# Graph attention and graph convolution on one core: three places for whole-array work in each batch instead of six

## The chip, the cores and the metric

The kernel runs on one core of a Trainium2 chip. The metric is the device time of one execution in microseconds (us). All data are 32-bit floats.

## The reference

`x` is (16, 1024, 256): 16 batches, 1024 nodes, 256 features. `adj` is (1024, 1024). Layer 0 is an attention whose queries come from a graph product, layer 1 a graph convolution with two linear layers and batch norms.

```python
# layer 0, with fea = x transposed to (b, c, n)
c_adj = mean(fea, axis=1)                              # mean of a node's features
diff  = c_adj[:, None, :] - c_adj[:, :, None]
A     = abs(abs(sigmoid(diff) - 0.5) - 0.5) * 2.0
Wg    = adj * (A + A.transpose(0, 2, 1)) * 0.5
g     = relu(einsum('bcn,bnm->bcm', fea, Wg) * para)
q     = g, as 4 heads of 64;   k, v = split(x @ kv_w)
out   = softmax(q k^T * scale) v
x     = layernorm(x + out)
# layer 1
A_hat = (adj + I) * dinv[:, None] * dinv[None, :]      # dinv = rsqrt(degree)
h     = relu(batchnorm((A_hat @ x) @ W1.T + b1))
x     = layernorm(x + batchnorm(h @ W2.T + b2))
```

## The kernel before

The function `fast_path` does the work in four stages: attention for all batches, aggregation with the first linear layer (with a seven-product scheme for block matrices), the second linear layer, and the final residual and layernorm. The change is in the first.

**The pieces of a batch.** The 1024 nodes lie as 8 chunks of 128. `prologue(b)` makes three lists of small steps for batch `b`, which the caller works off later:

- `first`: four `transpose_x(c, half)`, each of four 128x128 transposes on TensorE (tile `pxT`) and a copy to `xT`; the first of them also calls `begin`, which sums `x` on VectorE (`csum`), writes the negative means to memory and reads them back as a row on all partitions (`crow`).
- `side`: for each of 8 chunks `weights_abs` and `weights_tanh` on ScalarE and `weights_adj` on VectorE. They build the graph weights `wg` of 128x1024. That makes 24 steps.
- `steps`: four `values` (tile `pv`) and four `keys` (`pk`), and then `graph_mm`, the product of `x` with the 8 `wg` chunks (`pg`). At the end of each quarter `queries` multiplies with `para` on VectorE and applies Relu on ScalarE.

The profile counts each matmul of 32-bit data twice, so one quarter of `graph_mm` with its 8 matmuls is x16.

**The attention itself.** A unit is one batch, one pair of heads, one half of the queries (`qh`) and one chunk of keys (`m`). `scores(i)` makes the transposed scores of a unit (tile `ps`, from 64x64 quarters of the array) and their exponential `p` on ScalarE. `outputs(i)` multiplies `p` with the values (`po`, 64x64 quarters too) and sums `p` into `acc` on VectorE. A burst is two units; a batch has 16 bursts, with index `u` 0 to 15 in the batch. In each burst TensorE first makes the scores of burst `j` and then the outputs of burst `j-1` (`back`).

After each pair of heads `normalise` sums `acc` over partitions on TensorE (`den`, columns of 32), copies it on ScalarE (`drow`) and sends it through memory on SP's queue to come back as columns (`dcol`). `residual` takes the reciprocal, transposes the output (`poT`), multiplies (`o`) and adds to `x` on GpSimd. `finish_x1` does the layernorm and stores the result as `x1`.

**What sets the order.** The order on TensorE, ScalarE and VectorE is the order in which the loop emits the instructions (`manual_schedule`). Before the change whole-array work stands at these bursts, four steps at a time:

```python
FULL = (0, 4, 6, 8, 10, 12)
SIDE = {13: 2, 14: 2, 15: 2, 1: 2, 2: 2, 3: 2}
```

So `u` 0 and 4 hold values and keys (with two `side` steps behind each), and 6, 8, 10 and 12 one quarter of `graph_mm` each. 10 and 12 also take the transposes of the batch after next. `normalise` follows at the end of `u` 8 and, for the second pair, of `u` 0 of the next batch; the two `residual` of a pair four bursts later (`u` 12 and 4), `finish_x1` at `u` 5. The input of batch `b+2` is requested at `u` 5. In the last batch the free places hold the transposes of `adj` (`pah`) and of the layer-1 weights (`pw`).

**Buffers.** In PSUM the pool `s` has two tiles of two banks (scores), `t` two of one bank (`pxT`, `pv`, `pk`, `pg`, `den`, `poT`), and `o` two of one bank (`po`). In SBUF `p` has four buffers, `acc` two, `oT` three, `o` and `drow` one each, `x` three, `xT` and `crow` one, `wg` eight.

Of the kernel before, what the change touches and what calls it, by code (L numbers as in the profile page):

```python
# [18 lines left out]
P = 128  # L19
# [496 lines left out]
def fast_path(  # L516
# [86 lines left out]

    def products(name, bank, out, mm, temps, bias):
# [95 lines left out]
    with (  # L700
# [5 lines left out]
        tc.tile_pool(name="op", bufs=3) as op,  # L706
# [26 lines left out]
        def prologue(b):  # L733
# [24 lines left out]
            def transpose_x(c, half):  # L758
                if c == 0 and half == 0 and b:
                    begin()  # L760
# [7 lines left out]
                nc.vector.tensor_copy(s["xT"][:, c, half * HALF : (half + 1) * HALF], pt)  # L768
# [28 lines left out]
            def graph_mm(c, half, part):  # L797
                if part == 0:
                    s["pg"] = tile_t(f"pg_{b}_{c}_{half}")
                    if c == 0 and half == 0:  # L800
                        s["qT"] = qkv.tile([P, CC, N], F32, tag="qT", name=f"qT_{b}")
                ps = s["pg"]
                hs = slice(half * HALF, (half + 1) * HALF)
                for n in (2 * part, 2 * part + 1):
                    nc.tensor.matmul(  # L805
                        ps, xt[:, n, c * P : (c + 1) * P], s["wg", n][:, hs],
                        start=(n == 0), stop=(n == NCH - 1),
                    )
                if part == 3:
                    queries(c, hs, ps)  # L810
# [37 lines left out]
            def values(pair):  # L848
# [3 lines left out]
                for j in range(2):  # L852
# [6 lines left out]
                nc.vector.tensor_copy(  # L859
                    s["v"][:, 2 * pair : 2 * pair + 2, :].rearrange("p n c -> p (n c)"), pt  # L860
                )
# [3 lines left out]
            if b == 0:  # L865
                first += [(begin, ()), (row_of_means, ())]
            for i in range(4):
                step(values, i)
                step(keys, i // 2, i % 2)
            for c in range(CC):  # L870
                for half in range(2):
                    for part in range(4):
                        if b:
                            step(graph_mm, c, half, part)
# [105 lines left out]

        def finish_x1(b):
            xt = st.pop(b)["x"]
            layernorm(xt, f"l0_{b}")
            nc.gpsimd.dma_start(x1_d[b], xt)
# [125 lines left out]

        BURST = 2
        bursts = [range(i, i + BURST) for i in range(0, len(units), BURST)]
        PERB = PER // BURST
        FULL = (0, 4, 6, 8, 10, 12)
        SIDE = {13: 2, 14: 2, 15: 2, 1: 2, 2: 2, 3: 2}
        with tc.manual_schedule(engines={mybir.EngineType.PE, mybir.EngineType.Activation, mybir.EngineType.DVE}):
# [8 lines left out]
            run(next_first, 4)  # L1125
# [7 lines left out]
            full, sums, late = {}, {}, {}  # L1133

            def back(j):
# [4 lines left out]
                if m == NCH - 1 and qh == 1:  # L1140
                    sums.setdefault(j + 1, []).append((normalise, (b, pr)))
                    for q in range(2):
                        full.setdefault(j + 5, []).append((residual, (b, pr, q)))
                    if pr == PAIRS - 1:
                        late.setdefault(j + 6, []).append((finish_x1, (b,)))
# [14 lines left out]
                6: [(adjacency_rows, (n,)) for n in (0, 1, 2)] + [(load_weights, ())],  # L1160
                8: [(adjacency_rows, (n,)) for n in (3, 4, 5)],
                10: [(adjacency_rows, (n,)) for n in (6, 7)],
                12: [(adjacency_diagonal, ())],
            }
            for j in range(len(bursts)):
# [8 lines left out]
                run(late.get(j, []), 9)  # L1174
# [3 lines left out]
                if u in FULL:  # L1178
                    if u >= 10:
                        run(next_first, 1)  # L1180
                    for _ in range(4 if b or u > 4 else 0):
                        run(steps, 1)
                        if u <= 4:
                            run(side, 2)
                    if u >= 10:
                        run(next_first, 1)
                    run(full.get(j, []), 9)
                elif u > 12:
                    run(next_side, SIDE[u])
                else:  # L1190
# [441 lines left out]
```

## Time and profile before

| | |
|---|---|
| median of 3 runs | 2637.98 us (2637.81 to 2638.22) |
| the profiled execution | 2637.64 us, span 2635.9 us, mean TensorE clock 0.996 |
| TensorE matmul busy | 2572.7 us, 98% of the span |
| VectorE busy | 1587.8 us, 60% |
| ScalarE busy | 1110.2 us, 42% |
| GpSimd busy | 338.9 us, 13% |
| exponentials (512 on ScalarE) | 495.6 us, 1020 ns each |
| sums of `p` (384 of the 448 on VectorE) | 483.2 us, 1258 ns each |

The profile is of one execution. Times are from the start of its span. A group of instructions is written with its line, engine, operation, output and inputs, and count; in a timeline the first column is the start and the second the length. Matmuls overlap in the array and their ends are modelled, so distances between starts are the safer reading. A bracket gives the idle time of the engine before the group and what ended it. The queue of a wait is told as "engine line waited for: total us, times, longest us".

### The profile page before, as it was taken

The page shows a single profiled execution, that of the slowest core. Times are in us where ns is not written, and L with a number is a line of the kernel's source. Part 1 is how long each engine was busy: PE and PEld are TensorE (multiplying, and loading weights), DVE is VectorE, ACT ScalarE, POOL GpSimd, SP SyncE. Part 2 cuts the span into 40 slices and gives each one's busy share as a digit, 9 for nine tenths or more (in the row PEclk, how much of TensorE's full clock was granted, in tenths as well). Part 3 has the DMA queues.
Part 4 walks back from the last instruction along what each step waited for, and adds up shares of the span by engine and source line. Part 5 has one row for each costly group of instructions (what it writes and reads, how often), then busy time and mean ns, then how long its engine had stood idle before and what let it go on. Part 6 is the DMA issues. An engine that isn't in the chain of part 4 may idle for free. (4 is left out here: it accounts for less than half of the span.)

```text
span 2635.9 us, 32325 instructions
## 1 busy us (share of the span) xinstructions
PE 2572.7 (98%) x13158; PEld 1118.6 (42%) x13158; DVE 1587.8 (60%) x2159; ACT 1110.2 (42%) x1321; POOL 338.9 (13%) x407
## 2 busy tenths in 40 slices
PE   8999999999999999999999999999999999999986
PEld 4443444444434444444344443334444444444455
DVE  5465665756656657566566576766565565533367
ACT  5363563644635636546356364501100111133358
POOL 0001000100000001001000010232221122000036
PEclk9999999999999999999999999999999999999999
DMA  4001101011011010110110110112222222254458
GB/s 144 2 9 41 33 10 41 17 25 33 9 41 33 10 41 19 23 33 9 41 33 9 41 49 2 41 55 89 96 76 84 86 90 96 96 201 150 159 194 303
DMA packets 134557, 168.96 MB, mean 64 GB/s; under 512 B 86784, under 2 KB 120064, under 8 KB 124032
## 3 DMA queue, kind: packets, MB, share of 16 engines
q1 hardware_dynamic: 129568, 116.47, 14.1%
q0 software_dynamic: 4832, 50.34, 4.6%
q8 instruction: 105, 1.72, 0.3%
q14 instruction: 52, 0.43, 0.0%
HBM read 99.36 MB, written 67.44 MB: 63 GB/s over the span
## 5 line engine op out<-in xcount | busy, mean ns | idle before, releaser
L908 ACT ACTIVATE p<-ps 128x1024 f32<-128x1024 f32 x512 | 495.6, 1020 | 179.7 <-PE ps L903 132.6
L933 DVE TENSOR_TENSOR acc<-acc,p 128x1024 f32<-128x1024 f32 x384 | 483.2, 1258 | 60.9 <-ACT p L908 32.3
L903 PE MATMUL ps<-qT,kT 64*64 64x512 f32 x4096 | 490.5, 594 | 1.4 <-ACT p L908 1.4
L924 PE MATMUL po<-p,v 64*64 64x512 f32 x4096 | 485.3, 589 | 0.0
L805 PE MATMUL pg<-wg,x 128*128 128x512 f32 x960 | 425.2, 596 | 0.0
L979 POOL TENSOR_TENSOR x<-x,o 128x512 f32<-128x512 f32 x64 | 109.5, 1711 | 1434.8 <-DVE o L974 1434.8
L924 PEld LDWEIGHTS po<-p,v 64*64 64x64 f32 x4096 | 156.7, 133 | 282.8 <-issue 282.6
L805 PEld LDWEIGHTS pg<-wg,x 128*128 128x128 f32 x960 | 177.6, 190 | 226.9 <-issue 203.3
L903 PEld LDWEIGHTS ps<-qT,kT 64*64 64x64 f32 x4096 | 146.1, 132 | 280.2 <-issue 231.5
L817 ACT ACTIVATE qT<-qT 128x512 f32<-128x512 f32 x64 | 40.1, 630 | 481.9 <-DVE qT L814 481.9
L1457 PE MATMUL po<-hl,w12T 128*128 128x512 f32 x512 | 222.0, 596 | 3.6 <-ACT hl L1387 2.8
L814 DVE SCALAR_TENSOR_TENSOR qT<-pg,para_s 128x512 f32<-128x512 f32 x64 | 43.9, 689 | 270.7 <-PE pg L805 269.8
L793 DVE SCALAR_TENSOR_TENSOR wg<-wg,adj_s 128x1024 f32<-128x1024 f32 x128 | 153.1, 1217 | 16.0 <-ACT wg L789 16.0
L1457 PEld LDWEIGHTS po<-hl,w12T 128*128 128x128 f32 x512 | 97.7, 191 | 127.9 <-issue 120.4
L784 ACT ACTIVATE wg<-crow,ccol 128x1024 f32<-128x1024 f32 x128 | 146.6, 1146 | 12.2 <-DMA crow<-c 12.2
L789 ACT ACTIVATE wg<-wg 128x1024 f32<-128x1024 f32 x128 | 135.5, 1059 | 2.6
L1387 ACT ACTIVATE hl<-hl,bn_sh,bn_sg 128x1024 f32<-128x1024 f32 x64 | 74.4, 1229 | 137.4 <-DMA hl<-h 136.1
L855 PE MATMUL pv<-kvw_s,xT 128*128 128x256 f32 x512 | 124.0, 385 | 1.6 <-ACT kT L846 1.6
L1468 DVE TENSOR_SCALAR o<-po,col_b 128x1024 f32<-128x1024 f32 x31 | 39.8, 1283 | 138.1 <-PE po L1457 138.1
L842 PE MATMUL pk<-xT,kvw_s 128*128 128x512 f32 x256 | 120.3, 592 | 0.0
L855 PEld LDWEIGHTS pv<-kvw_s,xT 128*128 128x128 f32 x512 | 94.9, 190 | 51.9 <-issue 27.6
L1286 PE MATMUL b_agg<-aT,x1S 128*128 128x512 f32 x240 | 109.2, 598 | 0.0
(159 smaller groups left out, 2641.4 us busy)
## 6 DMA issues: line engine op xcount, KB each, us to landing
h<-hw POOLq DMA_DIRECT2D x16, 2048.0 KB, 6.6
hl<-h SPq DMA_DIRECT2D x15, 2048.0 KB
x<-x POOLq DMA_DIRECT2D x16, 1024.0 KB, 4.2
x1l<-x SPq DMA_DIRECT2D x16, 1024.0 KB
xf<-x SPq DMA_DIRECT2D x16, 1024.0 KB
out_dram<-o SPq DMA_DIRECT2D x16, 1024.0 KB
x<-in_x_dram SPq DMA_DIRECT2D x15, 1024.0 KB
crow<-c SPq DMA_DIRECT2D x15, 512.0 KB
```

The lines of the kernel that those rows point to most:

```text
L784: nc.scalar.activation(w, s["crow"], AF.Abs, bias=s["ccol"][:, n : n + 1])
L789: nc.scalar.activation(w, w, AF.Tanh, scale=0.5)
L793: nc.vector.scalar_tensor_tensor(w, w, 1.0, adj_s[:, n, :], op0=ALU.subtract, op1=ALU.mult)
L805: nc.tensor.matmul(ps, xt[:, n, c * P : (c + 1) * P], s["wg", n][:, hs], start=(n == 0), stop=(n == NCH - 1),)
L842: nc.tensor.matmul(ps, kvw_s[:, c, kc * P : (kc + 1) * P], s["xT"][:, c, hs], start=(c == 0), stop=(c == CC - 1),)
L855: nc.tensor.matmul(pt[:, j * C : (j + 1) * C], s["xT"][:, c, n * P : (n + 1) * P], kvw_s[:, c, C : 2 * C], start=(c == 0), stop=(c == CC - 1),
L903: nc.tensor.matmul(ps[kh * D : (kh + 1) * D, hd * HALF : (hd + 1) * HALF], kT[r, pr, ks], qT[r, pr, qh * HALF : (qh + 1) * HALF], start=Tr ...
L908: nc.scalar.activation(p, ps, AF.Exp)
L924: nc.tensor.matmul(g["po"][kh][hd * D : (hd + 1) * D, :], s["v"][r, m, h * D : (h + 1) * D], p[r, hd * HALF : (hd + 1) * HALF], start=(m = ...
L933: nc.vector.tensor_add(g["acc"], g["acc"], p)
L979: nc.gpsimd.tensor_tensor(xs, xs, o.rearrange("p n h d -> p n (h d)"), ALU.add)
L1457: nc.tensor.matmul(ps[:, hs], w2T[:, k, c * P : (c + 1) * P], h[k][:, hs], start=(k == 0), stop=(k == HC - 1),)
```

## The change

Whole-array work of a batch now stands at `u` 0, 4 and 8 only.

- `u` 0: seven of the eight value and key steps, two `side` steps behind each; `normalise` of the second pair of the batch before behind the second of them, and all four `residual` of that batch behind the third, fourth and sixth and at the end.
- `u` 4: the layernorm statistics of the batch before, then the first half of `graph_mm`, the layernorm's application in the middle of it, and the last key step.
- `u` 8: `begin` and two transposes of the batch after next, the second half of `graph_mm` with the other two transposes in its middle, and `normalise` of the first pair.
- `u` 9 to 15: one or two `side` steps behind each burst, ten in all; the other fourteen are those of `u` 0.

`graph_mm` now works on one 128-feature half with both halves of the columns, into a tile of the pool `s`; `queries` takes all 1024 columns at once. Half of the `xT` and `v` copies go to ScalarE (not for batch 0). The layernorm behind the attention is split by `layernorm_steps`: statistics on VectorE, two more small operations on GpSimd, and the application on ScalarE instead of VectorE. `oT` has four buffers. In the last batch the leftovers are placed by hand, and the row sums of `adj` are spread over more bursts of the batch before it.

```diff
+    def layernorm_steps(t, name):
+        st = small.tile([P, NCH, 6], F32, tag="ln_st", name=f"st_{name}")
+        mv = small.tile([P, NCH, 2], F32, tag="ln_mv", name=f"mv_{name}")
+        rstd = small.tile([P, NCH], F32, tag="ln_rs", name=f"rs_{name}")
+        nmr = small.tile([P, NCH], F32, tag="ccol", name=f"nm_{name}")
+        def statistics():
+            for n in range(NCH):
+                nc.vector.bn_stats(st[:, n, :], t[:, n, :])
+                nc.vector.bn_aggr(mv[:, n, :], st[:, n, :])
+            rsqrt(rstd, mv[:, :, 1], EPS)
+            nc.gpsimd.tensor_tensor(nmr, mv[:, :, 0], rstd, ALU.mult)
+            nc.gpsimd.tensor_scalar(nmr, nmr, -1.0, None, ALU.mult)
+        def apply():
+            for n in range(NCH):
+                nc.scalar.activation(
+                    t[:, n, :], t[:, n, :], AF.Identity,
+                    bias=nmr[:, n : n + 1], scale=rstd[:, n : n + 1],
+                )
+        return statistics, apply
...
-        tc.tile_pool(name="op", bufs=3) as op,
+        tc.tile_pool(name="op", bufs=4) as op,
...
             def transpose_x(c, half):
-                if c == 0 and half == 0 and b:
-                    begin()
...
-                nc.vector.tensor_copy(s["xT"][:, c, half * HALF : (half + 1) * HALF], pt)
+                copy = nc.scalar.copy if half and b else nc.vector.tensor_copy
+                copy(s["xT"][:, c, half * HALF : (half + 1) * HALF], pt)
...
-            def graph_mm(c, half, part):
-                if part == 0:
-                    s["pg"] = tile_t(f"pg_{b}_{c}_{half}")
-                    if c == 0 and half == 0:
+            def graph_mm(c, n):
+                if n == 0:
+                    s["pg"] = tile_s(f"pg_{b}_{c}")
+                    if c == 0:
                         s["qT"] = qkv.tile([P, CC, N], F32, tag="qT", name=f"qT_{b}")
-                ps = s["pg"]
-                hs = slice(half * HALF, (half + 1) * HALF)
-                for n in (2 * part, 2 * part + 1):
+                for hs in (H0, H1):
                     nc.tensor.matmul(
-                        ps, xt[:, n, c * P : (c + 1) * P], s["wg", n][:, hs],
+                        s["pg"][:, hs], xt[:, n, c * P : (c + 1) * P], s["wg", n][:, hs],
                         start=(n == 0), stop=(n == NCH - 1),
                     )
-                if part == 3:
-                    queries(c, hs, ps)
+                if n == NCH - 1:
+                    queries(c, slice(0, N), s["pg"])
...
-                nc.vector.tensor_copy(
-                    s["v"][:, 2 * pair : 2 * pair + 2, :].rearrange("p n c -> p (n c)"), pt
-                )
+                copy = nc.scalar.copy if pair % 2 and b else nc.vector.tensor_copy
+                copy(s["v"][:, 2 * pair : 2 * pair + 2, :].rearrange("p n c -> p (n c)"), pt)
...
+            else:
+                first.insert(0, (begin, ()))
...
-            for c in range(CC):
-                for half in range(2):
-                    for part in range(4):
-                        if b:
-                            step(graph_mm, c, half, part)
+            for c in range(CC if b else 0):
+                for n in range(NCH):
+                    step(graph_mm, c, n)
...
+        def statistics_x1(b):
+            statistics, st[b]["ln"] = layernorm_steps(st[b]["x"], f"l0_{b}")
+            statistics()
         def finish_x1(b):
-            xt = st.pop(b)["x"]
-            layernorm(xt, f"l0_{b}")
-            nc.gpsimd.dma_start(x1_d[b], xt)
+            s = st.pop(b)
+            s["ln"]()
+            nc.gpsimd.dma_start(x1_d[b], s["x"])
...
-        FULL = (0, 4, 6, 8, 10, 12)
-        SIDE = {13: 2, 14: 2, 15: 2, 1: 2, 2: 2, 3: 2}
...
-            run(next_first, 4)
+            run(next_first, 5)
...
                 if m == NCH - 1 and qh == 1:
-                    sums.setdefault(j + 1, []).append((normalise, (b, pr)))
+                    sums.append((normalise, (b, pr)))
                     for q in range(2):
-                        full.setdefault(j + 5, []).append((residual, (b, pr, q)))
+                        full.append((residual, (b, pr, q)))
                     if pr == PAIRS - 1:
-                        late.setdefault(j + 6, []).append((finish_x1, (b,)))
+                        late.append((statistics_x1, (b,)))
+                        late.append((finish_x1, (b,)))
...
             before_last = {
-                6: [(adjacency_rows, (n,)) for n in (0, 1, 2)] + [(load_weights, ())],
-                8: [(adjacency_rows, (n,)) for n in (3, 4, 5)],
-                10: [(adjacency_rows, (n,)) for n in (6, 7)],
-                12: [(adjacency_diagonal, ())],
+                6: [(load_weights, ())],
+                8: [(adjacency_rows, (n,)) for n in (0, 1, 2, 3)],
+                10: [(adjacency_rows, (4,))],
+                11: [(adjacency_rows, (5,))],
+                12: [(adjacency_rows, (6,))],
+                13: [(adjacency_rows, (7,))],
+                15: [(adjacency_diagonal, ())],
             }
...
                 if j:
                     back(j - 1)
-                run(late.get(j, []), 9)
                 if u == 5 and b + 2 < B:
                     load_x(b + 2)
                     next_first, next_steps, next_side = prologue(b + 2)
-                if u in FULL:
-                    if u >= 10:
-                        run(next_first, 1)
-                    for _ in range(4 if b or u > 4 else 0):
+                if b == B - 1:
+                    if u == 0:
+                        run(sums, 1)
+                    elif u in (2, 4, 12):
+                        run(full, 2)
+                    elif u == 5:
+                        run(late, 1)
+                    elif u == 7:
+                        run(late, 1)
+                    elif u == 8:
+                        run(sums, 1)
+                elif u == 0:
+                    for i in range(7):
+                        if b:
+                            run(steps, 1)
+                            run(side, 2)
+                        if i == 1:
+                            run(sums, 1)
+                        if i in (2, 3, 5):
+                            run(full, 1)
+                    run(side, 99)
+                    run(full, 1)
+                elif u == 4:
+                    run(late, 1)
+                    keys_last = steps[:1] if b else []
+                    del steps[: len(keys_last)]
+                    for n in range(NCH):
                         run(steps, 1)
-                        if u <= 4:
-                            run(side, 2)
-                    if u >= 10:
-                        run(next_first, 1)
-                    run(full.get(j, []), 9)
-                elif u > 12:
-                    run(next_side, SIDE[u])
-                else:
-                    run(side, SIDE.get(u, 0))
+                        if n == 3:
+                            run(late, 1)
+                    run(keys_last, 1)
+                elif u == 8:
+                    run(next_first, 3)
+                    for n in range(NCH):
+                        run(steps, 1)
+                        if n == 3:
+                            run(next_first, 2)
+                    run(sums, 1)
+                elif u > 8:
+                    run(next_side, 2 - u % 2)
                 if b == B - 2:
                     run(before_last.get(u, []), 9)
                 if b == B - 1:
                     run(last.get(u, []), 9)
-                run(sums.get(j, []), 9)
             j = len(bursts)
             back(j - 1)
             for m in range(NCH):
                 if m + 1 < NCH:
                     scale_adjacency(m + 1)
                 aggregate_first(m)
-                run(sums.get(j + m - 1, []), 9)
-                run(full.get(j + m, []), 9)
+                if m == 1:
+                    run(sums, 1)
+                if m == 4:
+                    run(full, 2)
             for i in range(NCH // 2):
                 adjacency_sums(i)
-            run(late.get(j + 5, []), 9)
+            run(late, 2)
```

More of the change, by code (lines that the diff above doesn't have):

```diff
@@ L1132, in fast_path @@
             run(next_steps, 8)
-            full, sums, late = {}, {}, {}
+            full, sums, late = [], [], []
             def back(j):
```

## The prediction

> **What bounds the kernel now.** I read the page's busy times first, then the instructions of TensorE in order of time over one middle batch, then its waits, then the other engines beside it.
>
> ```profile
> PE 2572.7 (98%) x13158; PEld 1118.6 (42%) x13158; DVE 1587.8 (60%) x2159; ACT 1110.2 (42%) x1321; POOL 338.9 (13%) x407
> PEclk9999999999999999999999999999999999999999
> ```
>
> TensorE has something in flight 98% of the span at full clock, so only what makes its instructions stand further apart than their work needs can be won. Busy time hides that, so I take starts. In the timeline of PE the columns are start, length, and group:
>
> ```profile
> 514.59 1.90 PE L903 MATMUL ps<-qT,kT 64*64 64x512 f32 x16
> 516.30 1.90 PE L924 MATMUL po<-p,v 64*64 64x512 f32 x16
> 518.13 7.13 PE L805 MATMUL pg<-wg,x 128*128 128x512 f32 x16
> 525.19 1.95 PE L903 MATMUL ps<-qT,kT 64*64 64x512 f32 x16
> 526.96 1.90 PE L924 MATMUL po<-p,v 64*64 64x512 f32 x16
> 528.68 1.90 PE L903 MATMUL ps<-qT,kT 64*64 64x512 f32 x16
> ...
> 547.80 7.03 PE L805 MATMUL pg<-wg,x 128*128 128x512 f32 x16
> 554.67 0.60 PE L765 MATMUL pxT<-ident,x 128*128 128x128 f32 x4
> ...
> 590.89 1.88 PE L842 MATMUL pk<-xT,kvw_s 128*128 128x512 f32 x4
> 592.70 1.06 PE L946 MATMUL den<-acc,ones 128*32 128x512 f32 x8
> 593.70 1.95 PE L903 MATMUL ps<-qT,kT 64*64 64x512 f32 x16
> ```
>
> Half a burst (ps or po, in 64*64 quarters of the array) takes 1.71 to 1.72 from start to start. The po before whole-array work takes 1.83 (516.30 to 518.13), 0.12 more. Sixteen pg take 7.06 if ps follows (518.13 to 525.19), and 6.87 if another whole-array group follows (547.80 to 554.67): 0.19 more. The first ps afterwards takes 1.77, 0.05 more. So one block of whole-array work between bursts costs 0.12+0.19+0.05 = 0.36 us beyond its work. A den (columns of 32) behind pk costs 0.10: 1.81 against the 1.71 between pk groups.
>
> Check on a whole batch: 16 bursts x 3.43 = 54.9; pg 4 x 6.87 = 27.5; eight value and key groups x 1.715 = 13.7; two den at 0.9, four pxT at 0.5, four poT at 0.55 = 6.0; waits 0.59; six blocks x 0.36 = 2.2. The sum is 104.9; the trace has 104.90 (pv at 502.69 to pv at 607.59). Nothing is left unexplained, and what can be won is blocks and waits, 2.8 us a batch.
>
> The waits of PE inside the attention part, and beside them the order on ACT in a block that holds keys and weights:
>
> ```profile
> PE poT L970 <- DVE qT L814: 5.2, 15, 0.3
> PE poT L970 <- ACT kT L846: 3.4, 14, 0.2
> PE ps L903 <- ACT p L908: 1.4, 2, 1.1
> ```
>
> ```profile
> 589.37 0.58 ACT L846 COPY kT<-pk 128x512 f32<-128x512 f32 x1 [2.09 <-PE pk L842]
> 589.85 1.15 ACT L784 ACTIVATE wg<-crow,ccol 128x1024 f32<-128x1024 f32 x1
> ```
>
> poT waits for one of the two buffers of the pool `t`: 0.24 when ACT must first empty the pk two groups earlier, 0.35 behind DVE's qT.
>
> **The change, part by part.**
>
> Blocks. Before: 4 in batch 0 (u 6, 8, 10, 12), 6 in each of batches 1 to 14, 6 in batch 15 = 94. After: 2 + 14 x 3 + 7 (poT alone at u 2 is a new one) = 51. 43 fewer x 0.36 = **15.5 us less**. Matmuls, weight loads and transposes stay the same in number.
>
> The den of the second pair moves from the end of a block to its inside (k, den, v). Leaving whole-array work into den is paid before and after; new is the return to v. Not shown before; nothing at least, 0.36 at most; the nearest row is the 0.10 of pk to den, with 0.1 more for a first pv (1.83 against 1.73): 0.2 x 14 = **2.8 more**. Here the Trainium skill (TensorEngine Tiling (Array Packing), Key Properties) says that changing the tiling mode drains TensorE, while another tile of the same mode does not. It agrees with transposes costing no step beside pg. Taken strictly, a 32-column den amid 128-column work is a full extra change, 0.36 x 14 = 5.0, and the forecast would be 2628.0. I take the row.
>
> Waits. The old 0.59 a batch goes (8.6 in all). In the new first block the order on `t` is v0, k0, den, v1, poT, k1, poT, v2, k2, poT, v3, poT. Three places have the known shape "ACT empties it, one poT in between": k1 behind v1, v2 behind k1, v3 behind k2, 0.24 each. ACT's order is abs, k0, tanh, drow, v1, abs, tanh, k1, abs, tanh, k2, abs, tanh, v3. From starts ACT takes 1.15 for an abs, 0.97 for a tanh, 0.48 for a copy. Laid against PE's 1.72 groups, ACT is free 0.9 before v1 is ready, 0.1 late for k1, 1.5 early for k2. So 0.72+0.1 = 0.82 x 14 = 11.5: **2.9 more** net. DVE's four o products now lie 2 to 4 us apart, so the single o buffer (POOL's 1.7 us add) no longer holds DVE; PE did not wait for that except in batch 15. dcol of the second pair: at the end of the attention DVE found it 3.9 us after the end of drow (1718.59 to 1722.51, the only DMA wait of that kind); here 8 us lie between.
>
> Weights and later DMAs. Ten side steps move to u 9 to 15: 1.2 us of ACT a burst beside 1.81 of exp, under 3.43. The oT copy fits too. begin now stands ahead of the third block. On SP, c to crow took 10.5 us from issue to issue (29.00 to 39.46) and 3.9 to land: with csum behind oT on DVE, crow lands about 18.3 us after the block starts, and ACT asks for it at 19.9. Cost nothing; cover 1.6 us, then some 0.5 before exp of the next burst is late. SP's den writes stand behind crow, ready at about the same time. The x load goes out behind the x1 store (u 5): store lands about 17 us after block two starts, the load took 5 us, x is needed at 29.5.
>
> Layernorm in two steps. DVE keeps 4.3 us of statistics, ACT gets eight Identity of 128x256. The nearest row, the same form with an SBUF source at the end (L1570), has 606 ns: 4.85 us at most; DVE's apply took 2.67. Against this stands the Trainium skill (ScalarE: Activation LUTs, Rules for kernel authors): use VectorE rather than ScalarE for multiply and add; its What ACT_TABLE_LOAD costs gives 280 + 0.833 N ns, 3.95 for eight as an estimate. By the rule the move loses 1.3 to 2.2 a batch, some 25 in all and 2651, if ACT were the limit there. It is not: block two keeps PE at pg and k3 for 15.6 us, in which ACT has only oT, this, one Relu and one copy, under 7 us. Nothing on the path. If that cover were gone, 4 us a batch. POOL's two new small operations (some 0.24 each) precede it.
>
> pg in pool `s` takes one of the two score buffers; its last matmul to the second score of the next burst is 1.73+0.86 (block two, k3 between) or 1.0+0.86 (block three, den between), the qT product of 1024 columns about 1.28 plus 0.2. Hidden by 0.4 at least. exp starts late behind Relu and drow in block three, but its buffers come free 0.5 before PE asks. xT and v copies on ACT lie in these slacks.
>
> Last batch. The exp held 3.94 by DVE's whole layernorm (1.08 on PE) goes; instead the ACT apply at u 7 holds exp and the adjacency copies about 1.5: **0.4 more**.
>
> End of attention:
>
> ```profile
> 1759.95 1.57 PE L1318 MATMUL b_h<-tT,w12T 128*128 128x512 f32 x2 [1.88 <-DVE u_h L615]
> 1761.31 4.90 PE L1286 MATMUL b_agg<-aT,x1S 128*128 128x512 f32 x8
> ```
>
> ```profile
> 1756.57 2.67 DVE L600 TENSOR_SCALAR x<-x,mv_l,rs_l 128x256 f32<-128x256 f32 x8 [2.11 <-POOL rs_l L589]
> 1759.15 0.74 DVE L615 SCALAR_TENSOR_TENSOR u_h<-b_h,col_b,p_h 128x512 f32<-128x512 f32 x1
> ```
>
> DVE waited for POOL and applied batch 15's layernorm ahead of u_h, and PE stood 1.88. That goes; ACT's agg copy is some 3.6 late instead, and its next reader is later still. Right after, eight b_agg took 4.74 to the next start instead of 3.43 (PEclk 0.57 from 1760 to 1764): 1.7 with b_h. Whether the dip goes too is open; half: 1.9+0.85 = **2.75 less**.
>
> Sum: -15.5 +2.8 +2.9 +0.4 -2.75 = -12.15. The profiled execution took 2637.64 (span 2635.9), 0.34 under the median of 2637.98, which I take as base: **2625.8**.
>
> **Rivals.**
> (a) The 0.36 is only partly per block, for instance because the ends of longer blocks stand further behind: half saved, 7.7, net 4.4: 2633.6. For it: the profile models matmul ends. Against: the batch sum closes at 104.9.
> (b) Slower: ACT paces the first block. If exp or weights leave ACT so far behind that two of the three copies (k1, k2) come one tanh (1.06) later, PE waits 2.1 more in 14 batches, 29.7: 2655. Deciding point: my gain of 0.7 a batch is gone once ACT is 0.8 late at k1. For it: only 0.1 of slack there. Against: ACT idles about 1.8 before k0.
> (c) The new waits don't come, den inside is free and the dip goes: 15.5+8.6+3.6 = 27.7, 2610. Against: the 0.24 was paid 14 times in this shape.
>
> **How the numbers follow.** My case 0.75, own range 2619 to 2631 (the bounds of den and dip, some 0.4 a batch on waits); (a) 0.12; (b) 0.08; (c) 0.05. 0.2%, 5.3 us, is what a measurement tells from no change; (a) lies within it. Faster 0.81, same 0.11, slower 0.08. The range 2617 to 2634 reaches into (a) and leaves out (b) and (c).
>
> **What would show it.** Right: a batch of about 104.15 from first pv to first pv; PE waits for ACT of 0.2 to 0.3 at k1, v2 and v3; no wait at poT; pg 13.7 for 32; no PE wait for u_h. Wrong: ps waiting for exp after block one or three, abs waiting for crow, or x late at the third block.

## The result and the profile after

The changed kernel takes 2630.41 us, the median of 12 runs (2629.23 to 2632.20), against 2637.52 for the kernel before, which ran beside it. The ratio is 0.9976, with a 95% interval of 0.9969 to 0.9984. The forecast was 2625.8, with a range of 2617 to 2634. The gain is 7.1 us where 12.15 were forecast: the sign held, the size came out at 0.6 of it. By its time alone the kernel lies nearer to rival (a) (2633.6) than to the forecast; what tells them apart are the timelines. The profiled execution has a span of 2628.9 us (2635.9 before).

The engines' busy times say little, as before:

```profile
PE 2565.4 (98%) x13158; PEld 1130.2 (43%) x13158; DVE 1515.3 (58%) x1941; ACT 1202.5 (46%) x1479; POOL 362.0 (14%) x439
```

VectorE went from 1587.8 to 1515.3 and ScalarE from 1110.2 to 1202.5, which is the layernorm's second half on its new engine and the shared copies. TensorE fell by 7.3, which is the size of the gain but does not show where it came from. For that I set stage starts from the timelines of TensorE against each other (us). A batch begins with its first `ps`. For batch 15 of the changed kernel, whose first `ps` come in pieces, the piece of twelve is taken (1621.88; the first single one starts 0.43 earlier). The last two starts are those of the first `pagg` and of the group behind the `b_agg` that follows the wait for `u_h`; the stretch between them, from the attention to the next stage, is the handover:

| stage | before | after | difference |
|---|---|---|---|
| first `ps` of batch 0 (prologue) | 75.46 | 75.86 | +0.40 |
| batch 0 | 86.99 | 85.25 | -1.74 |
| each of batches 1 to 13 | 104.90 | 104.41 | -0.50, together -6.47 |
| batch 14 | 104.45 | 103.48 | -0.97 |
| batch 15, to the first `pagg` | 77.57 | 81.76 | +4.19 |
| handover: `pagg` to the group behind that `b_agg` | 57.81 | 53.97 | -3.84 |
| from there to the end | 869.81 | 871.32 | +1.51 |

About 1 us of batch 0's gain and of batch 15's loss is the same work: the `poT` of each first pair moved on by one batch. The sum is -6.9, the difference of the spans (2635.86 and 2628.93). The middle batches fall short, the last batch loses, and the handover gains more than forecast.

First a middle batch: block one in the timeline of PE after the change (start, length, group, and the wait before it in brackets).

```profile
477.87 1.99 PE L877 MATMUL pv<-kvw_s,xT 128*128 128x256 f32 x8
479.70 1.88 PE L864 MATMUL pk<-xT,kvw_s 128*128 128x512 f32 x4
481.51 1.06 PE L967 MATMUL den<-acc,ones 128*32 128x512 f32 x8
482.51 1.99 PE L877 MATMUL pv<-kvw_s,xT 128*128 128x256 f32 x8
484.34 0.60 PE L991 MATMUL poT<-ident,oT 128*128 128x128 f32 x4
485.18 1.98 PE L864 MATMUL pk<-xT,kvw_s 128*128 128x512 f32 x4 [0.24 <-ACT v L882]
487.00 0.60 PE L991 MATMUL poT<-ident,oT 128*128 128x128 f32 x4
487.83 1.99 PE L877 MATMUL pv<-kvw_s,xT 128*128 128x256 f32 x8 [0.24 <-ACT kT L868]
489.67 1.88 PE L864 MATMUL pk<-xT,kvw_s 128*128 128x512 f32 x4
491.38 0.60 PE L991 MATMUL poT<-ident,oT 128*128 128x128 f32 x4
492.22 1.99 PE L877 MATMUL pv<-kvw_s,xT 128*128 128x256 f32 x8 [0.24 <-ACT kT L868]
494.05 0.60 PE L991 MATMUL poT<-ident,oT 128*128 128x128 f32 x4
494.58 1.95 PE L924 MATMUL ps<-qT,kT 64*64 64x512 f32 x16
```

The three forecast waits are there at the three forecast places, 0.24 each. But look at the starts, not at the brackets. The last `poT`, which nobody holds, takes 0.53 to the next start; those ahead of a wait take 0.84. And the group after a wait takes 1.82 (`pk`, 485.18 to 487.00) where an undisturbed one takes 1.71 (489.67 to 491.38). The bracket understates what the wait costs.

The other two blocks are as forecast:

```profile
508.48 14.00 PE L827 MATMUL pg<-wg,x 128*128 128x512 f32 x32
522.31 1.88 PE L864 MATMUL pk<-xT,kvw_s 128*128 128x512 f32 x4
524.12 1.95 PE L924 MATMUL ps<-qT,kT 64*64 64x512 f32 x16
```

32 `pg` take 13.83, and no `ps` waits behind them. On ScalarE, the layernorm's apply lies inside this block:

```profile
516.88 4.04 ACT L622 ACTIVATE x<-x,nm_l,rs_l 128x256 f32<-128x256 f32 x8 [7.70 <-POOL nm_l L618]
```

In the last batch one wait has grown and one is new, and no step of the prediction priced them. Ahead of the first stand the two `poT` with the single `o` buffer, ahead of the second `den` with its copy on ScalarE. First the row of the kernel before, then the two of the changed one:

```profile
1654.39 0.65 PE L1046 MATMUL pah<-ident,adj_s 128*128 128x128 f32 x4 [1.33 <-DVE o L974]
```

```profile
1648.83 0.66 PE L1071 MATMUL pah<-ident,adj_s 128*128 128x128 f32 x4 [1.90 <-DVE o L995]
...
1671.74 1.24 PE L1071 MATMUL pah<-ident,adj_s 128*128 128x128 f32 x8 [1.15 <-ACT drow L973]
```

At the handover the wait of 1.88 for `u_h` is gone, and so is the half clock behind it:

```profile
1753.32 1.02 PE L1373 MATMUL b_h<-tT,w12T 128*128 128x512 f32 x2
1754.18 3.60 PE L1341 MATMUL b_agg<-aT,x1S 128*128 128x512 f32 x8
```

`b_agg` takes 3.43 to the next start (4.74 before).

### The profile page after: what moved, and what is told of

Read it like the earlier page. It is cut to its first block, busy times and chain, and to the rows that moved or that the text cites. A ratio compares the mean times of both kernels' runs of the same rounds, so it can differ in the third digit from the quotient of the medians.

```text
span 2628.9 us, 32328 instructions
## 1 busy us (share of the span) xinstructions
PE 2565.4 (98%) x13158; PEld 1130.2 (43%) x13158; DVE 1515.3 (58%) x1941; ACT 1202.5 (46%) x1479; POOL 362.0 (14%) x439
## 3 DMA queue, kind: packets, MB, share of 16 engines
q8 instruction: 105, 1.72, 0.3%
## 4 chain that ended last, share of the span: by engine, by line
PE 83%; DVE 8%; ACT 6%; issue 1%; DMA 1%; POOL 0%; DVEq 0%; POOLq 0%; ACTq 0%
PE ps L924 16%; PE pg L827 16%; PE po L945 16%; PE po L1512 8%; PE pv L877 5%; PE b_agg L1341 4%; PE c_agg L1341 4%; PE pk L864 3%; PE b_h L1373 2%; PE a_agg L1341 2%; PE c_h L1373 2%; ACT o L1625 1%; ACT o L1554 1%; PE pxT L788 1%; PE den L967 1%
## 5 line engine op out<-in xcount | busy, mean ns | idle before, releaser
L1000 POOL TENSOR_TENSOR x<-x,o 128x512 f32<-128x512 f32 x64 | 123.1, 1924 | 1173.5 <-DVE o L995 1173.5
L924 PEld LDWEIGHTS ps<-qT,kT 64*64 64x64 f32 x4096 | 152.6, 133 | 282.7 <-issue 254.4
L836 DVE SCALAR_TENSOR_TENSOR qT<-pg,para_s 128x1024 f32<-128x1024 f32 (+1 forms) x34 | 39.2, 1160 | 236.2 <-PE pg L827 235.0
L817 DVE SCALAR_TENSOR_TENSOR wg<-wg,adj_s 128x1024 f32<-128x1024 f32 x128 | 162.1, 1278 | 22.9 <-ACT wg L813 22.9
L959 DVE TENSOR_TENSOR oT<-po,oT 128x512 f32<-128x512 f32 x64 | 44.2, 691 | 145.6 <-ACT oT L958 145.6
L622 ACT ACTIVATE x<-x,nm_l,rs_l 128x256 f32<-128x256 f32 x128 | 64.6, 587 | 111.4 <-POOL nm_l L618 111.4
```

The lines of the kernel that those rows point to most:

```text
L817: nc.vector.scalar_tensor_tensor(w, w, 1.0, adj_s[:, n, :], op0=ALU.subtract, op1=ALU.mult)
L924: nc.tensor.matmul(ps[kh * D : (kh + 1) * D, hd * HALF : (hd + 1) * HALF], kT[r, pr, ks], qT[r, pr, qh * HALF : (qh + 1) * HALF], start=Tr ...
```

## The experiments

Theories at the start. One: a block between bursts costs 0.36 us as forecast, and the shortfall lies in the ring of `t` (its two buffers, used in turn: each 0.24 costs more than 0.24) and in the order of the last batch. Two, the rival (a) of the prediction: a block is worth only half. Three, the rival (b): ScalarE is late in block one whatever the buffers are.

**e1_pot_o: the transposes of the output leave the ring.**

```diff
-        def residual(b, pr, qh):
+        def residual(b, pr, qh, bank=tile_t):
...
-            pt = tile_t(f"poT_{k}")
+            pt = bank(f"poT_{k}")
...
-                        full.append((residual, (b, pr, q)))
+                        full.append((residual, (b, pr, q) if b >= B - 2 else (b, pr, q, tile_o)))
```

> The changed kernel, with the four poT of the first block of batches 1 to 14 taken from the pool `o` (whose two po tiles were just emptied) and no longer from `t`; the first block's ring on `t` is then v0 k0 den v1 k1 v2 k2 v3. Theory one (the block price of 0.36 us was right, and what fell short of the forecast in batches 1 to 13 are the three waits of 0.24 us for a bank of `t` with 0.11 us of restart behind each): the three waits vanish, about 3 x 0.35 x 14 = 14.7 us, so about 2615.7 us and a batch period of about 103.4 us; the first block goes from 16.71 to about 15.7. Theory two (the block price was too high by half and the waits are as forecast, without a restart): only 3 x 0.24 x 14 = 10 us go, 2620. Theory three (ScalarE is late in the first block whatever bank is used): the waits turn up at other groups, within 2 us of the changed kernel.

Measured: 2631.83 us, ratio to the kernel before 0.998 (0.9973 to 0.9987), no gain on the changed kernel; batch period 104.47. Theories one and two miss the total. Theory three meets it, being within 2 us of the changed kernel, but not for its own reason, as the timeline of PE shows:

```profile
483.73 0.60 PE L991 MATMUL poT<-ident,oT 128*128 128x128 f32 x4
484.17 1.88 PE L864 MATMUL pk<-xT,kvw_s 128*128 128x512 f32 x4
...
491.93 0.60 PE L991 MATMUL poT<-ident,oT 128*128 128x128 f32 x4
492.46 1.95 PE L924 MATMUL ps<-qT,kT 64*64 64x512 f32 x16
494.23 1.02 PE L945 MATMUL po<-p,v 64*64 64x512 f32 x2
495.76 1.51 PE L945 MATMUL po<-p,v 64*64 64x512 f32 x11 [0.51 <-DVE o L995]
```

All three ring waits are gone and the new wait is for VectorE, so ScalarE is not late, and theory three falls. Block one takes 15.20 (16.71 in the changed kernel): 1.51 for three waits, 0.50 each, of which 0.40 lies before the group (0.84 against 0.44) and 0.10 in it. So theory one was right on the kind and still too low on the size. The gain is then lost again: `po` needs the bank of the last `poT`, which VectorE empties only behind two `wg` products. From this `ps` to the next `pg` are 15.47 us (492.46 to 507.93) where the changed kernel needs 13.90 (494.58 to 508.48). That is 1.57 for a wait whose bracket says 0.51.

**e2_last: another order in the last batch.** The transposes of `adj` stand ahead of `den` in bursts 0 and 8 and ahead of the residual in burst 4, the residual of burst 2 goes behind `den` in burst 0, and the apply from burst 7 to 9.

```diff
-                    if u == 0:
-                        run(sums, 1)
-                    elif u in (2, 4, 12):
-                        run(full, 2)
...
+                    if u in (0, 4, 8):
+                        run(last[u], 9)
+                    if u in (0, 8):
+                        run(sums, 1)
+                    if u in (0, 4, 12):
+                        run(full, 2)
+                    if u in (5, 9):
+                        run(late, 1)
```

> The changed kernel with another order in the last batch alone: the adjacency transposes go ahead of den in bursts 0 and 8, the residual of the first pair of the batch before moves from its own block at burst 2 to behind den at burst 0, the one at burst 4 behind the transposes, and the ScalarE apply of the layernorm goes from burst 7 to burst 9. Theory one (the last batch grew by 4.2 us, of which 1.1 is poT work moved on from the batch before and the rest a block of its own, den ahead, and two waits of pah of 1.90 and 1.15 us behind the o product and behind drow): 2 to 3 us less, about 2628; the waits of pah are gone, those of ps and pagg stay as they are. Rival (the last batch is held by VectorE and ScalarE work that only changes its place): less than 0.7 us.

Measured: 2625.42 us (2625.14 to 2625.97), ratio 0.9959 (0.9945 to 0.9972), 5.0 less than the changed kernel. The periods up to batch 14 are the same to 0.01; batch 15 takes 77.34 in place of 81.76. The waits of 1.90 and 1.15 are gone, and what is left there is short:

```profile
1646.24 1.23 PE L1071 MATMUL pah<-ident,adj_s 128*128 128x128 f32 x8 [0.34 <-ACT ahT L1074]
1647.68 1.24 PE L991 MATMUL poT<-ident,oT 128*128 128x128 f32 x8 [0.20 <-ACT ahT L1074]
```

That is more than expected. By the starts, bursts 0 and 2 give back 1.1 together, burst 8 0.95 and burst 4 2.4. At burst 4 this is more than the change had lost, as the kernel before stood there too (1.33 and 0.78). So the loss of the last batch was order, not work.

**e3_ln_vector: the layernorm's apply back on VectorE.**

```diff
...
-                nc.scalar.activation(
-                    t[:, n, :], t[:, n, :], AF.Identity,
-                    bias=nmr[:, n : n + 1], scale=rstd[:, n : n + 1],
-                )
+                nc.vector.tensor_scalar(
+                    t[:, n, :], t[:, n, :], mv[:, n, 0:1], rstd[:, n : n + 1],
+                    ALU.subtract, ALU.mult,
+                )
```

> The changed kernel with the second half of the layernorm (the apply, eight 128x256) back on VectorE as in the kernel before, at the same places; the two POOL products for its bias fall away. Theory one (the apply costs nothing on either engine in the middle batches, and on ScalarE it frees VectorE at the handover, where b_h waited 1.88 us for u_h): the batch period stays within 0.1 us of 104.4; the last batch loses its wait of pah for drow (1 us less); the handover is late by 1.9 us, and by up to 3.8 if the clock dip comes back there: 2631.5 to 2633.5 us. Rival (the apply on ScalarE delays the evictions of kT and v and so makes part of the waits): faster by over 2 us.

Measured: 2631.59 us, ratio 0.9979 (0.9971 to 0.9987); period 104.41, unchanged. In the middle batches the apply is free on either engine. In the last batch the wait of `pah` for `drow` is gone, as expected, but a stretch at half clock stands there instead (granted clock 0.57 from 1650 to 1654). At the handover, PE again waits:

```profile
1755.05 1.12 PE L1370 MATMUL b_h<-tT,w12T 128*128 128x512 f32 x2 [1.88 <-DVE u_h L637]
1756.01 5.29 PE L1338 MATMUL b_agg<-aT,x1S 128*128 128x512 f32 x8
```

Both parts of the old loss are back: 1.88 of waiting and 1.69 more in `b_agg`. Its stretch has the half clock (PEclk is the column after POOL):

```profile
1756.00:1760.00 4.00, 4.00 (x7) 1.69 (x6) 0.75 (x1) 0.00 (x0) 0.00 (x0) 0.57 0.60 240
```

Behind the handover this kernel is 3.5 us later than the changed one, at the end of the span 1.5: the changed kernel runs a stretch at half clock at 2316 to 2324, which this one does not have.

**e4_blocks: the kernel before with two graph blocks instead of four.** Eight half-steps of `pg` at burst 8 and eight at 12; `begin` stays at burst 10.

```diff
...
-        FULL = (0, 4, 6, 8, 10, 12)
+        FULL = (0, 4, 8, 12)
...
+                if u == 10 and next_first:
+                    st[b + 2]["begin"]()
                 if u in FULL:
                     if u >= 10:
-                        run(next_first, 1)
-                    for _ in range(4 if b or u > 4 else 0):
+                        run(next_first, 2)
+                    for _ in range(8 if u > 4 else 4 if b else 0):
...
```

> The kernel before, with only its graph products merged: eight half-steps of pg at burst 8 and eight at burst 12 in place of four at 6, 8, 10 and 12; the row of means still begins at burst 10, the four pxT stand around the block at burst 12. Two blocks of whole-array work fewer in each of batches 0 to 14, 30 in all; banks, layernorm and engines as before. Theory one (0.36 us for each block): 10.8 us less than the kernel before, 2626.7, with a batch period 0.7 us shorter than 104.90. Theory two (half of that, since the work merely drains elsewhere): 5.4 less, 2632. If a bank of `t` is late between pg and pxT, up to 0.35 us a batch (5 us) comes back, to be seen as a wait of pxT for VectorE's qT.

Measured: 2745.25 us, ratio 1.0413 (1.0399 to 1.0428): 107 us slower. As a test of the block price it failed, but it shows what the blocks are good for. In the timelines, PE's scores at burst 7, and then VectorE ahead of them:

```profile
550.20 3.69 PE L904 MATMUL ps<-qT,kT 64*64 64x512 f32 x16 [3.97 <-ACT p L909]
```

```profile
545.22 2.67 DVE L600 TENSOR_SCALAR x<-x,mv_l,rs_l 128x256 f32<-128x256 f32 x8 [2.12 <-POOL rs_l L589]
547.81 7.87 DVE L934 TENSOR_TENSOR acc<-acc,p 128x1024 f32<-128x1024 f32 x6
```

The layernorm at burst 5 keeps VectorE from `acc`, the four `p` buffers stay full, exp waits for VectorE, and TensorE for exp. In the kernel before, the `pg` block at burst 6 gave VectorE the 7 us to catch up; here no block follows. About a third of the loss is the clock behind each of these stands: the granted clock is 0.58 from 548 to 552 and 0.57 from 552 to 556, the `ps` takes 3.47 to the next start in place of 1.72 and the `po` behind it 2.70 in place of 1.83. That is 2.6 us in each of 14 batches. A further loss is a `pg` that waits 0.99 for the copies of two `pxT`. So a block is also the slack of the other engines. That the change can do with three because it puts statistics and apply around block two is inferred from this; no run moved them away.

**e6_k3_alone: the price of one block.** The last `pk` of a batch leaves its place behind `pg` and stands alone at burst 6.

```diff
-                    run(keys_last, 1)
+                elif u == 6:
+                    run(keys_last, 1)
```

> The changed kernel with one more block: the last keys group k3 no longer follows pg at burst 4, it stands alone at burst 6, in batches 1 to 14; nothing else moves. Theory one (a block between bursts costs 0.36: 0.12 at po, 0.10 at its first group, 0.10 at its last, 0.05 at the next ps): the period grows from 104.41 to 104.77, 5.0 us in all, 2635.4. Theory two (a block costs half of that, the rest was only the wait of the groups in it): 0.18, 2.5 us, 2632.9. Nothing else is expected to wait, since kT's last quarter is needed only in the next batch.

Measured: 2643.88 us (2641.45 to 2644.36), ratio 1.0025 (1.0016 to 1.0035); period 105.29, which is 0.89 more. The total is 13.5 us above the changed kernel where 5.0 were expected; 14 times 0.89 is 12.4 of it. Two places share the 0.89:

```profile
524.43 1.09 PE L924 MATMUL ps<-qT,kT 64*64 64x512 f32 x8
525.82 1.09 PE L924 MATMUL ps<-qT,kT 64*64 64x512 f32 x8 [0.30 <-DVE qT L836]
526.72 1.90 PE L945 MATMUL po<-p,v 64*64 64x512 f32 x16
...
530.16 1.90 PE L945 MATMUL po<-p,v 64*64 64x512 f32 x16
531.98 1.98 PE L864 MATMUL pk<-xT,kvw_s 128*128 128x512 f32 x4
533.90 1.95 PE L924 MATMUL ps<-qT,kT 64*64 64x512 f32 x16
535.66 1.90 PE L945 MATMUL po<-p,v 64*64 64x512 f32 x16
```

The lone `pk`: `po` ahead of it takes 1.82 (0.10 more than 1.72), it takes 1.92 itself (0.20 more than 1.71), and `ps` behind it 1.76 (0.05 more). That makes 0.36, as forecast; theory two falls. The other 0.52 was not expected: without `pk` between them, the second score asks for the bank of `pg` before VectorE has emptied it. `ps` to `po` is 2.29 instead of 1.77, 0.52 more, for a bracket of 0.30.

**e7_copies_vector: all copies of v and xT back on VectorE.**

```diff
-                copy = nc.scalar.copy if half and b else nc.vector.tensor_copy
+                copy = nc.vector.tensor_copy
...
-                copy = nc.scalar.copy if pair % 2 and b else nc.vector.tensor_copy
+                copy = nc.vector.tensor_copy
```

> The changed kernel with the evictions of v1, v3 and of the second halves of xT back on VectorE, as they all were before. Theory one (VectorE's queue in the first block holds weights of 1.2 us and o products, so v1 is emptied later than by ScalarE): k1 waits up to 1.2 us for v1 in place of 0.24, and the pg behind the first two pxT of the third block may wait up to 0.7 for xT: 0.5 to 2 us more a batch, 2637 to 2658. Rival (ScalarE is the busier of the two in the first block, so the three waits shrink): the waits of pv for kT go, the period falls by up to 1.0.

Measured: 2633.0 us, ratio 0.9984 (0.9978 to 0.9991); period 104.51, 0.11 more. Both sides missed the size. In the list of PE's waits in the attention, k1 (the second `pk`) waits 0.35 for VectorE in place of 0.24 for ScalarE, and no other wait moved:

```profile
PE pv L877 <- ACT kT L868: 6.7, 28, 0.2
PE pk L864 <- DVE v L882: 4.9, 14, 0.3
```

In the middle batches the sharing of these copies is worth 1.5 us in all (0.11 x 14). The total is 2.6 us above the changed kernel: batch 15 has a stretch at half clock here (granted clock 0.57 from 1650 to 1658) which the changed kernel does not have. Whether the copies bring it about was not tried.

**e5_three_o: the ring without its waits, and the last batch in order.** As e1_pot_o, but the last `poT` stays in `t`; with e2_last's order.

```diff
...
-                        full.append((residual, (b, pr, q)))
+                        full.append((residual, (b, pr, q) if b >= B - 2 or pr and q else (b, pr, q, tile_o)))
...
```

> The changed kernel with three of the four poT of the first block in the pool `o` and the last one left in `t`, and the order of the last batch of e2_last. Theory one (e1_pot_o took 1.51 us from the first block, since each reported wait of 0.24 delays the next start by 0.40 and lengthens the group after it by 0.10; it gave 1.57 back because the last poT sits in the bank that po needs and VectorE empties it only after two weights of 1.2 us): the first block takes 15.20, po behind the next ps starts at once, the batch period is 102.90; 14 x 1.51 + 5.0 us less than the changed kernel: 2604. Theory two (e1_pot_o's wait of po is VectorE's own lateness, which goes to the next thing that needs it): po or exp waits elsewhere and the period stays above 104.

Measured: **2603.63 us** (2602.96 to 2604.37), ratio to the kernel before 0.9875 (0.986 to 0.989): 34.0 us faster than the kernel before and 26.8 faster than the change. The period is 102.895, 1.51 less; batch 15 takes 77.34.

```profile
485.47 0.60 PE L991 MATMUL poT<-ident,oT 128*128 128x128 f32 x4
485.90 1.89 PE L877 MATMUL pv<-kvw_s,xT 128*128 128x256 f32 x8
487.63 0.60 PE L991 MATMUL poT<-ident,oT 128*128 128x128 f32 x4
488.16 1.95 PE L924 MATMUL ps<-qT,kT 64*64 64x512 f32 x16
489.93 1.90 PE L945 MATMUL po<-p,v 64*64 64x512 f32 x16
```

No bracket in the whole block, `po` follows `ps` after 1.77, and `pv` follows `poT` after 0.44. The forecast of 2604, made from e1's rows, holds; theory two of this run, that VectorE's lateness only moves on, falls.

**e8_ln_scalar: the kernel before with the split layernorm alone,** the apply on ScalarE at burst 6, behind that burst's outputs.

```diff
...
-                        late.setdefault(j + 6, []).append((finish_x1, (b,)))
+                        late.setdefault(j + 6, []).append((statistics_x1, (b,)))
+                        late.setdefault(j + 7, []).append((finish_x1, (b,)))
...
```

> The kernel before with the split layernorm alone: statistics on VectorE at burst 5, the apply on ScalarE at burst 6, ahead of the pg block there; blocks, banks and everything else as before. Theory one (in the middle batches the apply is hidden on either engine; at the handover to the next stage VectorE is late by it): the batch period stays 104.90; the wait of 1.88 us of b_h for u_h and the 1.7 us of the half clock behind it go, 3.6 us at the handover, of which a later half-clock stretch may take back up to 1.7: 2634 to 2636. Rival (the apply delays exp on ScalarE, since four us lie ahead of the exp of burst 7): ps waits for p once a batch, slower than the kernel before.

Measured: 2642.9 us, ratio 1.0024 (1.0015 to 1.0033), 4.8 us slower, a miss. The period is 104.98 (0.08 more), and the rival's wait for `p` did not come. The loss lies in the last batch, where burst 6 holds transposes of `adj` whose evictions stand behind the apply on ScalarE:

```profile
1673.77 1.97 PE L1075 MATMUL pah<-ident,adj_s 128*128 128x128 f32 x8 [4.94 <-ACT ahT L1078]
1675.67 3.43 PE L928 MATMUL ps<-qT,kT 64*64 64x512 f32 x16
```

The `ps` behind it runs at half clock as well. At the end of the attention this kernel is 9.7 us behind the kernel before, past the `b_agg` of the handover 5.9. The handover gains 3.8 here too, as in the changed kernel.

## Why the prediction was right, and where it was off

Between the forecast of -12.15 and the -6.9 of the spans lie 5.2 us: 2.0 in batches 1 to 14, 2.4 in batches 0 and 15 together (where the moved `poT` cancel), 1.5 behind the handover and 0.4 ahead of the first `ps`, both without a term; the handover gave 1.1 more than forecast, which hid part of it.

**Blocks, 0.36 each: held.** e6_k3_alone adds one and its rows pay 0.36. Nor do the ends of longer blocks cost more: block two, with 32 `pg`, costs 0.35 by its rows. Rival (a) is excluded. Two of the six removed places (`u` 10 and 12) begin and end in transposes and cost a little less: `po` to `pxT` 1.82, `pxT` to `pg` 0.49 against 0.44, `pxT` to `ps` 0.53. That makes 0.30 for them.

**den inside, +0.2 a batch: held.** The step into `den` takes 0.10 (1.81 against 1.71) and the return to `pv` 0.10 (1.83 against 1.73); the end of the block, with its own change, is still paid at the last `poT`. The Trainium skill (TensorEngine Tiling (Array Packing), Key Properties) says that a change of tiling mode drains TensorE. A change does cost something at every place here, but with `den` about 0.1 each way. The 0.36 that the strict reading would charge is a whole block with its change at `po` and `ps`.

**Waits, 0.82 new for 0.59 old: the mis-sized term.** Places and brackets were right (0.24, three times), and so was their cause. The step that failed is taking the bracket for the price. e1_pot_o and e5_three_o measure 0.50 for each, 1.51 a batch. The same reading holds for the two old waits in the rows of before:

```profile
509.68 0.60 PE L970 MATMUL poT<-ident,oT 128*128 128x128 f32 x4
510.52 0.66 PE L970 MATMUL poT<-ident,oT 128*128 128x128 f32 x4 [0.24 <-ACT kT L846]
...
569.59 0.60 PE L765 MATMUL pxT<-ident,x 128*128 128x128 f32 x4
570.54 1.26 PE L970 MATMUL poT<-ident,oT 128*128 128x128 f32 x8 [0.35 <-DVE qT L814]
```

The starts give 0.84 against 0.44, then 0.95 against 0.44, and with 0.26 in the groups behind them (0.59 against 0.53 and 1.18 against 0.97 to the next start) this makes 1.17, not 0.59. That the batch sum closed at 104.9 with 0.59 was luck: it took a transpose group at 0.5 or 0.55, where one that nobody holds takes 0.44, and so booked about the rest of the waits as work. The net is +0.34 where my terms had +0.23. What the blocks cost beyond their work is, by the same rows, 0.36, 0.35, 0.35, 0.36, 0.30 and 0.30 before (2.02), and 0.55 with den inside, 0.35 and 0.31 after (1.21). -0.81 and +0.34 give -0.47 a batch, against -0.50 measured and -0.65 by my terms. Of these 0.15 us the waits are 0.11. The "104.15" of the text was 0.1 lower than those terms.

**Weights, crow, x, `pg` in pool `s`: held at nothing.** No `ps` waits for exp and no ScalarE row waits for crow in the middle batches. The cover of the `pg` bank was thinner than it looked: e6_k3_alone takes `pk` away, and 0.52 appears.

**Layernorm on ScalarE: held.** Eight took 4.04, near the estimate of 3.95 worked out from the Trainium skill's figure (ScalarE: Activation LUTs, What ACT_TABLE_LOAD costs). Its rule to leave such work to VectorE (the same page, Rules for kernel authors) would have made it a loss; e3_ln_vector has the same period to 0.01, so in this place the choice costs nothing either way, and at the handover ScalarE is the better by 3.8. Where cover is missing, the rule's fear comes true: e8_ln_scalar paid 4.94 for one such place.

**Last batch, +0.4: wrong, +4.2.** This is the largest single error. By the starts it lies at four places, and 0.2 ahead of them. Burst 2 costs 1.2: the two `poT` moved on from batch 14, and 0.3 for their block, which I had counted. Burst 0 costs 1.25: `den` now stands ahead of `pah`, and its second half waits for VectorE's `acc` (bracket 0.29). Burst 8 costs 1.0, with `pah` behind `drow` and `drow` behind the apply, and burst 4 0.6 for the `o` buffer. What I did not walk through is the order of these steps; e2_last gives 4.4 back. The claim that "PE did not wait" for the single `o` buffer "except in batch 15" named the place and put no price on it: the bracket is 1.33 before and 1.90 after.

The rows of before were also misread here. The 3.94 of ScalarE and the 1.08 of TensorE do not come from the layernorm, which VectorE begins at 1657. They stand at 1626 and 1627, at the end of batch 14, where VectorE waits 1.28 for GpSimd ahead of an `o` product and then works 3.5 us on the diagonal of `adj` (L1033). That wait did go, but because the changed kernel spreads the work on `adj` over more bursts.

**Handover, -2.75: -3.8.** I gave the half clock one chance in two; it went. e3_ln_vector brings back both the wait and the half clock. But 1.5 us come back later: a stretch of half clock at 2532, which the kernel before does not have, takes 0.9 of it, and I had no term for that. Where the other 0.6 comes from stays open.

**Rivals (b) and (c):** (b) falls with e1_pot_o, in which ScalarE is in time for all three copies. Of (c), the half clock at the handover went, but the waits came.

## What to carry to other kernels

Price a wait by the starts of the groups around it, not by the number in the bracket: compare the interval with the same pair of groups undisturbed, and add what the next group takes longer. For short waits this matters most, as what comes on top of the bracket hardly grew with it here. Before changing what a short operation shares a ring with, write down the ring: a 0.44 us transpose between two 1.7 us groups leaves the evicting engine too little time, while another pool's idle bank costs nothing, provided the last user of that bank is early. Walk through the edge batch instruction by instruction, as it has its own neighbours, and before removing a block ask which other engine was catching up behind it.

## What the runs showed of the hardware

A wait cost TensorE its bracket and about a quarter of a us more: 0.50 for 0.24 (the changed kernel), 0.52 for 0.30 (e6_k3_alone), 0.61 for 0.35 (e7_copies_vector, 0.948 against 0.436 and 0.10 in the group behind), 1.37 for 1.08 (the kernel before at 1627) and 2.01 for 1.77 (the changed kernel's `b_h` at 1742.95). The rows show where it lies: an undisturbed `poT` has length 0.60 but 0.44 to the next start, so 0.16 of overlap is lost in a wait that is counted from its end, and the group behind takes 0.10 longer.

The exception is 1.57 for 0.51 in e1_pot_o, where two of the 16 `po` had started and the others were held. Up to the next block, the timeline then shows `ps` and `po` in interleaved pieces (x1, x3, x12), which reads as quarters of the array that no longer run in step, and the last `po` ahead of the block takes 0.40 more (2.23 against 1.83). The same pieces stand at the end of batch 14 in the changed kernel (1612.86 to 1625.65). There no bracket stands in the stretch, and yet it is 0.66 longer than seven undisturbed halves of bursts; the cause stays open.

The clock falls to half for about 3.4 us, in some places 6.8 (e7_copies_vector from 1650), after some waits of 1.9 us and not after others. The same `pah` wait of 1.90 stands in the changed kernel and in e1_pot_o, and these are the four us around it (the last column but two is PEclk), first in the changed kernel, then in e1_pot_o:

```profile
1648.00:1652.00 4.00, 2.25 (x15) 1.56 (x16) 2.65 (x5) 1.73 (x5) 2.81 (x3) 1.00 0.00 0
```

```profile
1648.00:1652.00 4.00, 2.33 (x12) 1.81 (x12) 2.60 (x6) 1.34 (x4) 2.74 (x3) 0.81 0.00 0
```

The clock stays at 1.00 in one and falls in the other (0.81, and 0.76 in the four us after), which costs about 1.7 us. What decides it was not tried. For a kernel whose gain is 7 us, a few such stretches are a visible part of what one run differs from another.
